# Two shared-expert blocks change their place in a two-layer mixture-of-experts kernel

## The chip, the cores and the metric

The kernel runs on one core of one Trainium2 chip. The metric is device time in microseconds of one execution. The core has a matrix engine (TensorE, PE in the profile, with its weight loads as PEld), a vector engine (VectorE, DVE), a scalar engine (ScalarE, ACT), GpSimd (POOL) and a queue that issues most DMA transfers (SyncE, SP). Each engine works through its own instructions in order and waits on semaphores for the others. Matrix products land in PSUM; everything else lives in SBUF or, for large intermediate tensors, in DRAM.

## The reference, cut to what matters

4096 tokens of width 256 go through a feed-forward layer, an attention layer and the same feed-forward layer again, each added to its input (the feed-forward layers by half). A feed-forward layer is a mixture of eight routed experts plus a shared expert that sees all tokens:

```python
logits = xn @ router_w.T                      # per token, after an RMS norm
topk_p, topk_i = jax.lax.top_k(softmax(logits), 2)
dispatch = order[:, :capacity]                # up to 640 tokens of each expert
xg = xf[dispatch]
eout = einsum('eci,eih->ech', silu(xg @ rg) * (xg @ ru), rd)   # inner width 1024
routed = zeros.at[dispatch].add(eout * weight)
shared = silu(x @ sg) * (x @ su) @ sd         # inner width 2048, all tokens
return shared + routed

x = x + 0.5 * ffn(layernorm(x))
x = x + attn(layernorm(x))                    # 16 heads, causal, groups of 64 tokens
x = x + 0.5 * ffn(layernorm(x))
```

The shared expert and the routed experts of a layer both only add to the output, so they may run in any order once their inputs are there.

## The kernel before

Tokens are cut into 32 tiles of 128 and eight blocks of 512. Weights and activations are split in two 16-bit planes (high and low), and each product is formed from three of the four combinations, so every matrix product appears three times.

**Work units.** A *front* (`front_steps`, L606) takes one tile: layer-norm statistics, the two planes into a tile `X` that also carries four numbers for routing, a DMA transpose of them into the block's `xb`, and the router's logits (L207). Phase a has ten buffers for `X` (the `10` in L751), phase c has six. After a block's fourth tile, `route` (L214) finds each token's two experts and places (`di`, L266), and `scatter` (L279) writes each of the four `X` tiles with two indirect DMAs from POOL into the experts' lists `xg` in DRAM; only then is the `X` buffer free. A *shared block* (`shared`, L349) runs the shared expert over one block of 512 tokens in 16 chunks of the inner width. A chunk is `gate_up` (L296): twelve products of 128x512 into `pgu`, the activation on ACT, a multiply on DVE, a cast to `hh` on ACT and a subtraction to `hl` on DVE. Then comes `down`: twelve products of 128x256 into `po`, put off by one chunk (`defer`), so that the chain on ACT and DVE runs beside the next chunk's products. With `tanh=True` the activation is put together from tanh with one more DVE operation[...]. After the last chunk the residual, loaded at chunk 2 by `res_load`, is added (L363) and stored (L366). The routed experts (`experts`, L389) go over eight experts in eight chunks each, with weights loaded and split on the fly, and end each expert with five scaled tiles `eo` (four buffers) that POOL adds to the output by indirect DMA (L426).

**Phases.** Phase a interleaves the 32 first-layer fronts with shared blocks 0 to 4 of the first layer (`NA = 5`). Phase b runs the first layer's experts. Phase c runs the attention tiles (`attn_tile`, L473, each with the second layer's front at its end) among shared blocks: first-layer blocks 5 to 7, then second-layer blocks 0 to 7. Phase d runs the second layer's experts, whose results are added to the output itself; the kernel ends there.

**What sets the order.** `drive` (L677) takes steps of a shared block, three for each chunk, and after every `RATE` of these lets all live tiles go on by one step, which is a slot; a tile starts every `GAP` slots. With `RATE_A = 3.0` a slot is one chunk. `run_slots` moves tiles alone when a block has to wait for its fronts. This order is then rearranged within each engine by a scheduler at build time; on the chip it is fixed. In phase a the residual rows of the blocks that are not done there are copied from `x` to `acc`, one 512 KB copy each (L764 and L765). The attention writes its result to a DRAM tensor `x2`, from which second-layer blocks load their residual.

Of the kernel before, what the change touches and what calls it, by code (L numbers as in the profile page):

```python
# [27 lines left out]
NB = 8  # L28
BT = 512
# [8 lines left out]
class Net:  # L38
# [307 lines left out]
            res.append(r)  # L346
        return res

    def shared(self, b, xb, src, dst, tanh=False, res=None):  # L349
        nc = self.nc  # L350
        outs = [self.ps_out.tile([P, BT], F32, name="po", tag="po") for _ in range(2)]
        for c in range(16):
            if c == 2 and res is None:
                res = self.res_load(src, b)
            h = self.hbuf()
            yield from self.gate_up(self.sgu[:, c], xb, h, tanh)

            def fin(c=c, h=h):
                self.down(outs, 4, h, self.sdw[:, :, c], c, 16)
                if c < 15:  # L360
                    return
                for i in range(2):
                    nc.vector.scalar_tensor_tensor(  # L363
                        out=res[i], in0=outs[i].rearrange("p (t f) -> p t f", f=H), scalar=0.5 / WS,
                        in1=res[i], op0=ALU.mult, op1=ALU.add)
                    nc.sync.dma_start(  # L366
                        out=dst[b * BT + i * 2 * P:b * BT + (i + 1) * 2 * P].rearrange("(t p) f -> p t f", p=P),
                        in_=res[i])

            self.defer(fin)  # L370
            yield
# [299 lines left out]
def run_slots(tiles, until):  # L671
    while not until():
        for _ in tiles.steps():
            pass


def drive(main, tiles, rate):  # L677

    credit = 0.0
    side = iter(())  # L680
    for _ in main:
        credit += 1.0
        for _ in range(2):
            if next(side, "end") == "end":
                break
        if credit >= rate:
            for _ in side:
                pass
            credit -= rate
            if not tiles.done():  # L690
                side = tiles.steps()
    for _ in side:
        pass


@with_exitstack
def macaron(ctx, tc, x, w_qkv, ln_w, w_proj, router_w, rg, ru, rd, sg, su, sd, out):
    nc = tc.nc
    x = x.rearrange("b s h -> (b s) h")
    out = out.rearrange("b s h -> (b s) h")  # L700
    n = Net(ctx, tc)
    R1 = n.route_init(0)
    R2 = n.route_init(1)
    R2["acc"] = out
    x2 = n.dr.tile([T, H], F32, name="x2")
    fbs = {}
    used = set()

    def new_fb(h, b):
        def get(t):  # L710
            if t == 0:
                assert h == 1 or (1, b) in used
                fb = fbs[(h, b)] = n.front_new()
                fb["pe"] = h == 1 and b < PEB
            return fbs[(h, b)]
        return get

    def tail(R, h, b, t):
        if t == 3:
            yield from n.route(R, b, fbs[(h, b)])  # L720

    def tile1(j):
        b, t = divmod(j, 4)
        y = n.load_tile(x, b, t)
        yield
        yield
        yield from n.front_steps(y, t, new_fb(1, b))
        yield from tail(R1, 1, b, t)

    def tile2(j):  # L730
        b, t = divmod(j, 4)
        yield from n.attn_tile(R1, j, x2, new_fb(2, b))
        yield from tail(R2, 2, b, t)

    def ready(h, b):
        return lambda: (h, b) in fbs and fbs[(h, b)]["n"] == 4

    def all_shared(key, b, src, dst, **k):
        yield from n.shared(b, fbs[key]["xb"], src, dst, **k)
        used.add(key)  # L740

    def fill(R):

        for e in range(E):
            z = n.raw.tile([P, 5, XW], F32, name="zero")
            nc.gpsimd.memset(z, 0.0)
            nc.vector.tensor_scalar_add(z[:, :, H], n.tokid[:, 0:5], float(T + e * CAP))
            nc.sync.dma_start(out=R["xg"][e * CAP:(e + 1) * CAP].rearrange("(t p) f -> p t f", p=P), in_=z)
            yield

    with n.phase("a", BT, 2, 10):  # L751
        n.ident = n.at.tile([P, P], F32, name="ident")
        make_identity(nc, n.ident)
        n.load_router(router_w)
        tiles = Tiles(tile1, 32, GAP_A)
        run_slots(tiles, ready(1, 0))
        n.load_shared(sg, su, sd)
        for _ in fill(R1):
            pass
        for b in range(NA):  # L760
            run_slots(tiles, ready(1, b))
            if b == 2:
                tiles.extra.append(fill(R2))
                for i in range(NA, NB):  # L764
                    nc.sync.dma_start(out=R1["acc"][i * BT:(i + 1) * BT], in_=x[i * BT:(i + 1) * BT])  # L765
            drive(all_shared((1, b), b, x, R1["acc"]), tiles, RATE_A)
        run_slots(tiles, tiles.done)
        cur = {}
        for _ in n.expert_load(R1, 0, cur):
            pass  # L770
    with n.phase("b", CAP, 3):
        n.experts(R1, rg, ru, rd, cur)
    with n.phase("c", BT, 2, 6, SLC):
        n.attn_init(w_qkv, ln_w, w_proj)
        tiles = Tiles(tile2, 32, GAP_C)
        for b in range(NA, NB):
            drive(all_shared((1, b), b, R1["acc"], R1["acc"], tanh=True), tiles, RATE_C)
        for b in range(8):
            run_slots(tiles, ready(2, b))
            drive(all_shared((2, b), b, x2, R2["acc"], tanh=True), tiles, RATE_C)  # L780
        run_slots(tiles, tiles.done)
        cur = {}
        for _ in n.expert_load(R2, 0, cur):
            pass
    with n.phase("d", CAP, 3):
        n.experts(R2, rg, ru, rd, cur)


NA = 5
RATE_A = 3.0  # L790
GAP_A = 2
RATE_C = 3.0
GAP_C = 4
# [32 lines left out]
```

## Time and profile before

Three timed runs gave a median of 1871.48 us (1870.2 to 1871.99). The profiled execution took 1875.79 us, of which 1874.1 are the span from its first to its last instruction.

| what | value |
|---|---|
| time of three runs, median | 1871.48 us |
| profiled execution, its time and its span | 1875.79 us, 1874.1 us |
| mean granted TensorE clock | 0.994 |
| matmuls | 13546 |
| first matmul of the first layer's experts | 361.45 us |
| share of the 16 DMA engines' time taken by SP's queue, by POOL's | 41.1%, 6.6% |
| HBM read and written | 80.52 MB, 52.33 MB |

The page gives a chain of waits, followed back from the last instruction. Its shares by engine say what the span was made of:

```profile
PE 57%; DVE 12%; POOL 10%; issue 9%; DMA 6%; ACT 4%; SPq 2%; POOLq 0%; DVEq 0%; ACTq 0%
```

"issue" is time in which an engine waited for nothing that the profile shows. A row of a timeline reads: start in us, length in us, engine, line, operation, output and inputs, size and count, and in brackets how long the engine was idle before and what released it.

### The profile page before, as it was taken

How to read it: one execution, taken by the hardware profiler on the slowest of the kernel's cores; microseconds unless marked ns; L12 is line 12 of the kernel's file. 1: busy time of each engine (PE TensorE's matmuls, PEld its weight loads, DVE VectorE, ACT ScalarE, POOL GpSimd, SP SyncE). 2: the span in 40 equal slices, each digit the busy share in tenths (PEclk: the TensorE clock that was granted, in tenths of full speed). 3: DMA queues.
4: the chain of work that ended last, by engine and by line, in shares of the span. 5: the costliest groups of instructions: out<-in, count | busy, mean ns of one | idle time of the engine just before them, and what ended most of it. 6: DMA issues, size and time to landing. Idle time of an engine off the chain costs nothing.

```text
span 1874.1 us, 37396 instructions
## 1 busy us (share of the span) xinstructions
PE 1786.8 (95%) x13546; PEld 1191.7 (64%) x13546; DVE 1262.5 (67%) x3190; ACT 942.1 (50%) x1991; POOL 724.5 (39%) x943
## 2 busy tenths in 40 slices
PE   6899999999999999999999999999999999999996
PEld 3455555677777765666565655656566567777775
DVE  8756554456666656788888888888886556565663
ACT  5323323355555535666566666656643335555553
POOL 5743332011112223455757667575753001111122
PEclk9999999999999999999999999999999999999998
DMA  9742113045455424556657576766631304544542
GB/s 278 220 125 75 35 29 86 21 102 115 112 113 125 104 55 86 110 105 120 139 114 141 102 141 119 135 121 119 129 62 37 86 12 102 114 113 105 117 109 50
DMA packets 447481, 196.07 MB, mean 105 GB/s; under 512 B 302353, under 2 KB 444365, under 8 KB 447248
## 3 DMA queue, kind: packets, MB, share of 16 engines
q1 hardware_dynamic: 429632, 172.51, 41.1%
q0 software_dynamic: 17664, 21.17, 6.6%
q8 instruction: 106, 1.74, 0.4%
q14 instruction: 79, 0.65, 0.1%
HBM read 80.52 MB, written 52.33 MB: 71 GB/s over the span
## 4 chain that ended last, share of the span: by engine, by line
PE 57%; DVE 12%; POOL 10%; issue 9%; DMA 6%; ACT 4%; SPq 2%; POOLq 0%; DVEq 0%; ACTq 0%
PE pgu L306 36%; PE po L330 19%; POOL xg L287 3%; DVE hl L322 2%; DVE sl L319 2%; DVE sl L314 2%; DMA xg<-X,di 1%; DMA QT<-QK 1%; DMA rs<-in_L_ffn_su_dram 1%; POOL X L285 1%; DMA y<-in_L_attn_x_dram 1%; ACT hh L321 1%; POOL e L561 1%; DVE st L139 1%; POOL S L550 1%
## 5 line engine op out<-in xcount | busy, mean ns | idle before, releaser
L306 PE MATMUL pgu<-xb,sgu 128*128 128x512 f16 x3072 | 738.8, 380 | 26.3 <-DVE sl L319 11.1
L321 ACT CAST hh<-sl 128x512 f16<-128x512 f32 (+2 forms) x512 | 272.8, 533 | 563.3 <-DVE sl L319 521.4
L306 PE MATMUL pgu<-xe,wc 128*128 128x384 f16 (+1 forms) x3072 | 497.0, 299 | 0.5
L306 PEld LDWEIGHTS <-sgu 128*128 128x128 f16 x3072 | 293.2, 98 | 301.1 <-issue 35.8
L319 DVE SCALAR_TENSOR_TENSOR sl<-pgu,sl 128x512 f32<-128x512 f32 (+2 forms) x512 | 300.2, 587 | 204.7 <-PE pgu L306 171.4
L322 DVE TENSOR_TENSOR hl<-sl,hh 128x512 f16<-128x512 f32 (+2 forms) x512 | 328.4, 642 | 154.4 <-ACT hh L321 147.5
L330 PEld LDWEIGHTS <-hh 128*128 128x128 f16 x3328 | 320.6, 98 | 115.0 <-ACT hh L321 17.9
L306 PEld LDWEIGHTS <-wc 128*128 128x128 f16 x3072 | 300.5, 98 | 94.1 <-issue 1.8
L330 PE MATMUL po<-sdw,hh 128*128 128x256 f16 x2048 | 351.9, 273 | 7.3 <-ACT hh L321 6.9
L330 PE MATMUL po<-sdw,hl 128*128 128x256 f16 x1024 | 251.9, 274 | 15.8 <-DVE hl L322 10.8
L330 PE MATMUL po<-wd,hh 128*128 128x256 f16 x1280 | 223.4, 273 | 0.0
L330 PEld LDWEIGHTS <-hl 128*128 128x128 f16 x1664 | 162.9, 98 | 67.4 <-DVE hl L322 27.2
L317 ACT ACTIVATE sl<-pgu 128x384 f32<-128x384 f32 (+1 forms) x336 | 159.0, 473 | 55.3 <-PE pgu L306 34.2
L426 POOL DMA_INDIRECT out_dram<-eo,eid x40 | 64.6, 1616 | 313.8 <-DVE hl L322 248.3
L287 POOL DMA_INDIRECT xg<-X,di x128 | 136.0, 1063 | 112.2 <-DVE di L266 54.1
L426 POOL DMA_INDIRECT acc<-eo,eid x40 | 65.1, 1627 | 285.4 <-DVE hl L322 245.8
L330 PE MATMUL po<-wd,hl 128*128 128x256 f16 x640 | 152.4, 273 | 2.1 <-DVE hl L322 2.1
L314 DVE SCALAR_TENSOR_TENSOR sl<-sl,pgu 128x512 f32<-128x512 f32 x176 | 119.9, 681 | 38.3 <-ACT sl L313 37.2
L100 ACT ACTIVATE wc<-re 128x512 f16<-128x512 f32 x128 | 80.5, 629 | 83.3 <-PE pgu L306 52.9
L313 ACT ACTIVATE sl<-pgu 128x512 f32<-128x512 f32 x176 | 103.9, 591 | 33.3 <-PE pgu L306 31.8
L101 DVE SCALAR_TENSOR_TENSOR wc<-re,wc 128x512 f16<-128x512 f32 x128 | 88.3, 690 | 26.6 <-ACT wc L100 26.4
L550 POOL TENSOR_TENSOR S<-S,amx 128x1024 f32<-128x1024 f32 x32 | 63.7, 1990 | 81.3 <-DVE amx L549 74.4
(140 smaller groups left out, 1719.6 us busy)
## 6 DMA issues: line engine op xcount, KB each, us to landing
re<-in_L_ffn_rg_dram SPq DMA_DIRECT2D x128, 128.0 KB
re<-in_L_ffn_ru_dram SPq DMA_DIRECT2D x128, 128.0 KB
re<-in_L_ffn_rd_dram SPq DMA_DIRECT2D x128, 128.0 KB
xg<-zero SPq DMA_DIRECT2D x16, 650.0 KB
y<-acc SPq DMA_DIRECT2D x64, 128.0 KB
y<-in_L_attn_x_dram SPq DMA_DIRECT2D x32, 128.0 KB
acc<-xr SPq DMA_DIRECT2D x16, 256.0 KB
x<-y SPq DMA_DIRECT2D x32, 128.0 KB
```

The costliest lines, as they stand in the source:

```text
L101: nc.vector.scalar_tensor_tensor(out=lo, in0=src, scalar=WS, in1=hi, op0=ALU.mult, op1=ALU.subtract)
L287: i = nc.gpsimd.indirect_dma_start(out=R["xg"][:, :], out_offset=bass.IndirectOffsetOnAxis(ap=di[:, t, k:k + 1], axis=0), in_=X, in_offset ...
L306: nc.tensor.matmul(p, lhsT=wc[:, w, i, k, :], rhs=x[:, 2 * a + k, :], start=(j == 0), stop=(j == 5))
L313: nc.scalar.activation(s, p, AF.Tanh, scale=0.5 / XP)
L314: nc.vector.scalar_tensor_tensor(out=s, in0=s, scalar=1.0, in1=p, op0=ALU.add, op1=ALU.mult)
L317: nc.scalar.activation(s, p, AF.Silu, scale=1.0 / XP)
L319: nc.vector.scalar_tensor_tensor(out=s, in0=ps[1], scalar=1.0 / XP / (2.0 * XP if tanh else 1.0), in1=s, op0=ALU.mult, op1=ALU.mult)
L321: nc.scalar.copy(h[0], s)
L322: nc.vector.tensor_tensor(out=h[1], in0=s, in1=h[0], op=ALU.subtract)
L330: nc.tensor.matmul(o, lhsT=h[a][:, t * P:(t + 1) * P], rhs=wd[:, w], start=(c == 0 and j == 0 and t % 2 == 0), stop=(c == nch - 1 and j == 2),
L426: i = nc.gpsimd.indirect_dma_start(out=R["acc"][:, :], out_offset=bass.IndirectOffsetOnAxis(ap=ids[:, t:t + 1], axis=0), in_=eo, in_offset ...
L550: self.anchor = nc.gpsimd.tensor_tensor(out=S, in0=S, in1=mx.unsqueeze(2).to_broadcast([P, 16, 64]), op=ALU.subtract)
```

## The change

Three things change together.

- `NA` goes from 5 to 4 and `RATE_A` from 3.0 to 2.5. Phase a keeps four shared blocks; first-layer block 4 moves to the start of phase c, where it takes the tanh form, with its residual rows copied to `acc` beforehand like those of blocks 5 to 7. A slot of phase a shrinks to 2.5 steps, 0.83 of a chunk.
- A new constant `NC = 7` leaves second-layer block 7 out of phase c and runs it in phase d, behind the routed experts and with the plain Silu form. Its residual is loaded at chunk 10 instead of 2 (`late=10`).
- The attention tiles of block 7 write their result to `out` instead of `x2`; the experts add to these rows, and the moved block loads them from `out` and stores them back. Since phase d's `h` buffers are 640 wide, `shared` cuts them to 512.

```diff
-    def shared(self, b, xb, src, dst, tanh=False, res=None):
+    def shared(self, b, xb, src, dst, tanh=False, late=2):
...
-            if c == 2 and res is None:
+            if c == late:
                 res = self.res_load(src, b)
-            h = self.hbuf()
+            h = [a[:, 0:BT] for a in self.hbuf()]
...
-        yield from n.attn_tile(R1, j, x2, new_fb(2, b))
+        yield from n.attn_tile(R1, j, x2 if b < NC else out, new_fb(2, b))
...
-        for b in range(8):
+        for b in range(NC):
             run_slots(tiles, ready(2, b))
             drive(all_shared((2, b), b, x2, R2["acc"], tanh=True), tiles, RATE_C)
...
         n.experts(R2, rg, ru, rd, cur)
+        for b in range(NC, NB):
+            for _ in all_shared((2, b), b, out, out, late=10):
+                pass
...
-NA = 5
-RATE_A = 3.0
+NA = 4
+NC = 7
+RATE_A = 2.5
```

## The prediction, made before the changed kernel ran

> **What bounds the kernel now.** I read the page's busy times first, then the rows by slice, then busy time by stage, then the end and the first stage in order of time.
>
> ```profile
> PE 1786.8 (95%) x13546; PEld 1191.7 (64%) x13546; DVE 1262.5 (67%) x3190; ACT 942.1 (50%) x1991; POOL 724.5 (39%) x943
> ```
>
> TensorE is busy for 95% of the span and no other engine for over 67%. So the time is TensorE's work plus its gaps, 87.3 us in all. The table by stage (columns: stretch, its length, then busy time and instructions of PE, PEld, DVE, ACT, POOL, granted clock, DMA share, GB/s) shows where these are. The stretches are phase a, b, c, d and what follows the last matmul.
>
> ```profile
> 0.00:363.00 363.00, 328.78 (x2062) 192.86 (x2063) 210.87 (x735) 124.12 (x227) 143.96 (x282) 0.99 0.40 110
> 363.00:683.00 320.00, 319.58 (x2529) 247.11 (x2527) 193.88 (x419) 168.25 (x398) 59.91 (x42) 1.00 0.46 104
> 683.00:1544.00 861.00, 827.48 (x6489) 510.40 (x6489) 665.46 (x1622) 483.14 (x974) 454.45 (x574) 1.00 0.54 104
> 1544.00:1857.20 313.20, 311.01 (x2471) 241.29 (x2468) 191.36 (x415) 165.78 (x393) 58.40 (x41) 1.00 0.46 106
> 1857.20:1874.10 16.90, 0.00 (x0) 0.00 (x0) 0.89 (x2) 0.83 (x2) 7.75 (x5) 0.61 0.36 39
> ```
>
> The gaps are 34.2 us in a (15.4 of them in the first 25 us), 0.4 in b, 33.5 in c, 2.2 in d, and 16.9 behind the last matmul. The two expert phases are full; only a, c and the end have anything to give.
>
> **The moved blocks.** A shared block is 16 chunks of 24 matmuls. The chain of waits shows the same group of a bare chunk return every 3.90 us:
>
> ```profile
> 336.92 2.16 PE pgu L306 x10
> 340.82 2.16 PE pgu L306 x10
> ```
>
> So a block is 16 x 3.90 = 62.4 us of TensorE. Phase a loses one (block 4), c loses one (2,7) and gains one (1,4), d gains one. The matmuls are the same in number and shape: the sum is 0. Phase c keeps eleven blocks, all with the tanh form, for 32 attention tiles. In the built programs every engine's sequence from the attention weights to the last expert is the same one instruction by instruction, except for names of tensors (the residual of one block now comes from `acc` instead of `x2`, four stores go to `out`). Last logits stand 25.5 chunks ahead of phase d's start in both. So I cost b and c at 0: their stalls stay, among them the two per block that c shows around each route.
>
> **The end.** Today the last matmul ends at 1857.2, and five scatters leave POOL one by one:
>
> ```profile
> 1857.81 1.55 POOL L426 DMA_INDIRECT out_dram<-eo,eid  x1 [27.70 <-DVE eo L425]
> 1859.67 1.54 POOL L426 DMA_INDIRECT out_dram<-eo,eid  x1 [0.30 <-issue]
> ...
> 1861.69 0.48 DVE L425 TENSOR_SCALAR eo<-po,ew 128x256 f32<-128x256 f32 x1 [4.08 <-DMA out_dram<-eo,eid]
> ...
> 1865.22 1.56 POOL L426 DMA_INDIRECT out_dram<-eo,eid  x1 [0.31 <-issue]
> ```
>
> They are issued by 1866.8 and the span ends 7.3 us later, at 1874.1. In the changed kernel they stand under the appended block. Its own end is two residual adds and two stores:
>
> ```profile
> L363 DVE SCALAR_TENSOR_TENSOR xr<-po,xr x32: 678/681/692, 99.4 to 1543.2; 128x512 f32<-128x512 f32 x32
> ```
>
> ```profile
> 1012.20 2.63 DMA out_dram<-xr
> ```
>
> The three numbers behind the colon are the shortest, median and longest add in ns; the second line is a landing of such a store in the chain of waits.
>
> The first add starts about 0.4 us before the last matmul ends (four matmuls of the other half follow its operand), so the second ends 1.0 us after; issue 0.4, landing 2.6, and 1.4 for the closing waits and barriers (0.6 of waits on SP and 0.75 from POOL's last drain to the end, by today's trace): 5.4 us instead of 16.9, **-11.5**. Bounds of the end: 4 us if the second store lands faster, 12 if POOL's closing drain, which today ends 6.5 us behind its last scatter, comes on top; it should be over, since POOL has by then been idle for some 50 us. The last chunk has no successor to hide its chain (multiply 0.69, cast 0.62, subtract 0.64 against 1.3 us of the earlier down products): **+0.4**.
>
> **Expert to shared block in d.** Expert 7's fifth `eo` has to wait for the first scatter's landing (4.08 us above; four buffers), and DVE is in order: the `sl` and `hl` of chunk 1 stand behind it. TensorE can run on for about a chunk on the three PSUM tiles of `pgu`. Nearest rows: between experts, with the same wait, TensorE loses 0 to 1.2 us; at the start of c, experts to a tanh block, 2.6. Silu has one DVE operation less than tanh, so between: **+1.5**, ends 0 and 4. The residual load at chunk 10 waits on SP for all scatters; only the two final stores are queued behind it, and 39 us have gone by against some 12 for five scatters: 0.
>
> **The denser front (phase a).** Rate 2.5 puts 28 fronts and eight routes over 50 chunks instead of 60; TensorE's cover for them shrinks, the work stays. What stalls today is a ring: each tile takes one of ten `X` tiles, and its cast on ACT waits until the tile ten before it was scattered.
>
> ```profile
> ACT X L164 <- DMA xg<-X,di: 25.4, 14, 3.0
> PE pgu L306 <- DVE sl L319: 9.0, 8, 2.5
> ```
>
> The columns are us in total, waits, and the longest. The casts wait 25.4 us on ACT, and TensorE is idle for 12.6 us from 75 to 250. From the first scatter's start to the release of tiles 0 to 3 of a block takes 4.0, 6.5, 9.1 and 11.6 us (165.78 to the casts at 169.75 and 172.31, then two scatters of 1.28 each per tile): 1.0, 1.7, 2.3, 3.0 chunks. The built order puts the casts 2,2,3,3 chunks behind `di` for tiles 10-13 and 14-17, 1,2,2,3 for the next three groups, 1,2 for tiles 30 and 31. After: 3,4,4,4; 1,2,2,3; 1,1,2,2; 1,2,2,3; 1,2,3,3; 1,1. The largest shortfall per group sums to 0.9 chunks before and 2.3 after: 1.4 chunks, 5.5 us more of ACT waiting. By today's ratio 12.6 / 25.4 half of it reaches TensorE: +2.8.
>
> Here a rule weighs in. TensorE is granted half its clock for windows of 3.4 us:
>
> ```profile
> 105.61 0.59 PE L306 MATMUL pgu<-xb,sgu 128*128 128x512 f16 x2 [2.00 <-DVE sl L319]
> 147.75 1.03 PE L330 MATMUL po<-sdw,hh 128*128 128x256 f16 x4 [0.28 <-ACT hh L321]
> ```
>
> Four products take 1.03 us at 147.75, behind a wait of 2.51, and 0.60 elsewhere; the granted clock is 0.93 from 100 to 125. The Trainium skill ("TensorE: Matmul & The Clock Gate", section "HAM oscillation — how this bites in real kernels") puts the danger at idle gaps above about 3.4 us. By the rule, longer waits of 2 to 3 us cost only themselves: +2.8. By the row a wait of 2.0 to 2.5 already loses half a window, 1.7 us. Not each does: 1.91 us at 686.75 was followed by full clock. I go by the row and allow 0.4 of one more window, 0.7. Phase a: **+3.5**. Low end -3 (stalls such as 105.61, where DVE waited for a load of `y`, need not recur); high end +14, the second rival below. One more 512 KB copy to `acc` is issued near 29 us, where the DMA engines are full (share 1.16): 1.8 us at 287 GB/s, but TensorE is busy throughout that slice, so 0 within these ends.
>
> At the end of a the last `di` stands 11 chunks ahead of the first expert instead of 17: 43 us. Today the last block's scatters start at 297.4 and the weights of the first two expert chunks are split by 323.7, so 26.3 suffice: 16 spare, and ACT's order puts the first split 4 chunks behind `di` in both.
>
> **Sum.** -11.5 + 0.4 + 1.5 + 3.5 = -6.1. Against the profiled span of 1874.1 (its run took 1875.8, 1.7 around it) that is 1868.0; the median of the runs, 1871.5, becomes **1865.4**. A change under 0.2%, 3.7 us, can't be told from none.
>
> **Rivals.**
> - *The front costs nothing* (0.20): a neutral or better a, -1, leaves -10.6: 1860.9. For it: groups 10-13 get more slack, and the scheduler placed the order knowing the rate. Against: groups 18-21 and 30-31 get less.
> - *Gain given back* (0.18): 4 at the expert boundary and 7 in a: -11.5 + 0.4 + 4 + 7 = -0.1, 1871.4. For it: DVE is in order behind a 4 us wait, at a place no trace shows.
> - *The X ring becomes the bound* (0.16), the slower side. Place: the casts on ACT behind the scatters. If each of five groups adds a wait of 2.5 us and a half-clock window of 1.7, a grows by 21: 1871.5 - 9.6 + 21 = 1882.9. It decides from 13.3 us in a (9.6 of gain and 3.7). For it: POOL takes a fixed 10 us for eight scatters, while a block's turn (8 slots, of 1 chunk before and 0.83 after) falls from 31 to 26 us. Against: 26 still holds them, with DVE at 27 of 50 us and DMA at 0.23 share from 200 to 250.
> - That the experts start late is inside the last: it takes over 16 us of slip.
>
> The forecast itself has 0.46, from 1862 to 1868. Faster: 0.46 + 0.20 = 0.66; same 0.18; slower 0.16. Range 1859 to 1877: below lies little of the second case, above about two thirds of the slower one.
>
> **What would show it.** Last matmul to end: near 5.4 us. First expert matmul near 361.5 - 62.4 + 3.5 = 302.6. Phases b and c as long as now, within 2 us. TensorE's gap at the expert boundary 0 to 4 us. I am wrong if a keeps more than 13 us of its 62.4, if c changes length, or if a POOL drain still follows the last store.

## The result

Four timed runs of the changed kernel have a median of 1853.26 us (1851.16 to 1854.37), four of the kernel before 1870.84. The ratio is 0.9907, with a 95% interval of 0.9895 to 0.992: 17 us faster, and 6 us below the lower end of the predicted range. A second set of runs gave the unaltered changed kernel 0.9924 (0.9911 to 0.9937), which is 14 us; one of its six runs, 2309.23 us at a granted clock of 0.753, is a slow one and left out. So the gain lies between 14 and 17 us where 6.1 were forecast.

The profiled execution took 1854.02 us, its span is 1852.2. The page's busy times, and the first of its shares of the chain of waits:

```profile
PE 1785.9 (96%) x13546; PEld 1189.7 (64%) x13546; DVE 1259.6 (68%) x3190; ACT 940.6 (51%) x1991; POOL 726.0 (39%) x943
...
PE 59%; DVE 11%; POOL 9%; DMA 8%; issue 6%; ACT 4%; SPq 1%; DVEq 0%; POOLq 0%; ACTq 0%
```

TensorE does the same 13546 matmuls in the same time. Its gaps were 87.3 us of the span and are 66.3. The table by stage of the changed kernel, with phases a, b, c, d, the appended block, and what follows the last matmul:

```profile
0.00:292.00 292.00, 264.46 (x1667) 153.82 (x1668) 183.87 (x700) 103.42 (x194) 145.43 (x282) 0.99 0.50 134
292.00:607.00 315.00, 314.86 (x2505) 244.40 (x2503) 192.73 (x415) 166.64 (x394) 58.43 (x41) 1.00 0.46 105
607.00:1466.00 859.00, 826.67 (x6476) 508.43 (x6475) 665.01 (x1622) 482.29 (x973) 455.93 (x574) 1.00 0.53 104
1466.00:1783.00 317.00, 315.39 (x2505) 244.28 (x2503) 192.72 (x416) 167.83 (x395) 58.32 (x41) 1.00 0.45 105
1783.00:1847.90 64.90, 64.56 (x401) 38.73 (x399) 24.39 (x38) 20.41 (x35) 7.89 (x5) 1.00 0.12 19
1847.90:1852.20 4.30, 0.00 (x0) 0.00 (x0) 0.86 (x2) 0.00 (x0) 0.00 (x0) 0.86 0.37 122
```

The gaps are now 27.5 us in a (34.2 before), 0.1 in b, 32.3 in c (33.5), 1.6 in d, 0.3 in the appended block and 4.3 at the end (16.9). Two places gave the time: the end and phase a. With the stages cut at the first and last gate or up product of each layer's experts, the two profiled executions stand like this:

| stretch | before, us | after, us | difference | predicted |
|---|---|---|---|---|
| a: start to the first expert product | 361.45 | 291.84 | -69.6 = -62.4 - 7.2 | -62.4 + 3.5 |
| b: first layer's experts | 315.4 | 314.9 | -0.5 | 0 |
| c | 860.8 | 859.0 | -1.8 | 0 |
| d: second layer's experts | 317.3 | 316.9 | -0.4 | 0 |
| last gate or up product of an expert to the end | 19.1 | 69.5 | +62.4 - 12.0 | +62.4 - 9.6 |

The pair of profiles differs by 21.8 us, 4 to 8 more than the timed runs. The profiled execution before was a long one: its 1875.79 us lie above all four timed runs of its kernel here (1868.89 to 1871.99). The chip counts too: the four sets of experiments, each on another chip, put the median of the kernel before at 1868.48, 1867.83, 1871.1 and 1876.16 us, and on which chip this profile was taken is not on record. So times are compared within a set only, and part of the -7.2 in phase a may belong to that one execution, which the experiments have to settle.

**The end.** The last rows of the changed kernel in order of time (start, length, engine and line, operation, and in brackets the idle time before and what ended it):

```profile
1846.10 0.61 PE L330 MATMUL po<-sdw,hh 128*128 128x256 f16 x4 [0.20 <-ACT hh L321]
...
1847.47 1.29 DVE L363 SCALAR_TENSOR_TENSOR xr<-po,xr 128x512 f32<-128x512 f32 x2 [0.70 <-PE po L330]
...
1847.60 0.27 PE L330 MATMUL po<-sdw,hl 128*128 128x256 f16 x1
1848.19 0.98 SPq L366 DMA_DIRECT2D out_dram<-xr  x2
```

No POOL instruction stands here any more. The last matmul ends at 1847.87, the two adds at 1848.8, the second store is issued and landed, and the span ends 4.28 us behind the last matmul instead of 16.9. The last chunk's bare chain costs the 0.20 in the first row.

**Experts to the shared block in d.** The same view where the last scatters now run:

```profile
1787.45 3.83 PE L306 MATMUL pgu<-xb,sgu 128*128 128x512 f16 x17
1788.15 1.70 POOL L426 DMA_INDIRECT out_dram<-eo,eid  x1 [30.44 <-DVE eo L425]
...
1792.16 0.48 DVE L425 TENSOR_SCALAR eo<-po,ew 128x256 f32<-128x256 f32 x1 [3.75 <-DMA out_dram<-eo,eid]
1792.43 0.81 PE L306 MATMUL pgu<-xb,sgu 128*128 128x512 f16 x3
```

DVE does wait 3.75 us for the first scatter with its fifth `eo`, but TensorE runs 17 gate and up products in one go under it and shows no wait at all. Its three PSUM tiles of cover were enough.

### The profile page after: what moved, and what is told of

The parts are those of the page before. It is cut to its first block, busy times and chain, and to the rows that moved or that the text cites. A ratio compares the mean times of both kernels' runs of the same rounds, so it can differ in the third digit from the quotient of the medians.

```text
span 1852.2 us, 37412 instructions
## 1 busy us (share of the span) xinstructions
PE 1785.9 (96%) x13546; PEld 1189.7 (64%) x13546; DVE 1259.6 (68%) x3190; ACT 940.6 (51%) x1991; POOL 726.0 (39%) x943
## 4 chain that ended last, share of the span: by engine, by line
PE 59%; DVE 11%; POOL 9%; DMA 8%; issue 6%; ACT 4%; SPq 1%; DVEq 0%; POOLq 0%; ACTq 0%
PE pgu L306 38%; PE po L330 19%; POOL xg L287 3%; DVE hl L322 2%; DVE sl L319 2%; DMA xg<-X,di 2%; DVE sl L314 2%; DMA xg<-zero 1%; DMA y<-in_L_attn_x_dram 1%; DMA rs<-in_L_ffn_su_dram 1%; POOL X L285 1%; ACT hh L321 1%; DMA QT<-QK 1%; DVE st L139 1%; ACT V L554 1%
```

## The experiments

Two theories stood against each other at first. *Ring*: phase a pays for its density through the ten `X` tiles, so the surplus must come from elsewhere. *Front*: the denser front itself gains. The edits are against the kernel named with each. Ratios are to the kernel before on the same chip, in the same set of runs.

### First set: the parts of the change one by one

**front_only.** The kernel before with the denser front alone.

```diff
-RATE_A = 3.0
+RATE_A = 2.5
```

> The kernel before with RATE_A 2.5 alone; five blocks stay in phase a, eight second-layer blocks in phase c. The prediction's theory (the ring of X tiles makes a denser front dearer): phase a longer by 3.5 us, so about 1874. Rival one (the gaps of phase a come once per front or route and are bounded by what TensorE meets there, so that fewer chunks beside fronts means fewer gaps): phase a shorter by 3 to 7 us, 1864 to 1868. Rival two (phase a's gaps vary from run to run and the rate means nothing): within 2 us of before.

Measured 1866.68 us, ratio 0.9988 (0.998 to 0.9997): a gain of 2 us, at the limit of what can be told. The +3.5 of the forecast had the wrong sign; a gain of 3 to 7 was too much as well.

**no_late_block.** The changed kernel with block 7 back in phase c.

```diff
-NC = 7
+NC = 8
```

> The changed kernel with NC 8: four blocks in phase a and the denser front, but all eight second-layer blocks in phase c, so the kernel ends with the last expert's scatters as before. If the end is worth the 11.5 to 12.6 us that the two traces show, this runs 12 to 13 us slower than the changed kernel, 1865 to 1866, and what is left against before (5 us) belongs to phase a. If the late block gains by something else as well (phase c being shorter at its end), the difference is larger.

Measured 1865.76 us, ratio 0.9982 (0.9975 to 0.9989): 3 us for the whole front part. Against the changed kernel's 0.9907 and 0.9924 the appended block is thus worth 14 or 11 us; its trace ends 19.1 us behind the last expert product, as before.

**late_only.** The changed kernel with phase a as it was.

```diff
-NA = 4
+NA = 5
...
-RATE_A = 2.5
+RATE_A = 3.0
```

> The changed kernel with NA 5 and RATE_A 3.0: phase a as before, block (2,7) moved behind the experts, ten blocks left in phase c. The end gains 12 us as in the changed kernel. Phase c loses a block of cover: the last logits stand 9.5 chunks (37 us) ahead of the second experts instead of 25.5, and route, scatters and expert load took some 35 us in the trace of before. If that cover suffices, 1858 to 1859; if it falls short, TensorE is idle at the start of phase d by 5 to 15 us and the time is 1863 to 1873.

Measured 1858.33 us, ratio 0.9954 (0.994 to 0.9968), a gain of 9 us by the ratio and 10 by the medians. Its trace has the changed kernel's end (69.6 us behind the last expert product). But its phase a, the same order of work as before, took 356.72 us where the profile before shows 361.45. TensorE's idle time in phase a was 34.2 us there and is 32.4 here, and a window of half clock comes three times there and once here. So one execution can make 4.7 of the -7.2 by itself, and 2.5 are left for the change.

**four_slow_front.** The changed kernel with the old rate.

```diff
-RATE_A = 2.5
+RATE_A = 3.0
```

> The changed kernel with RATE_A 3.0: four blocks in phase a but the front as thin as before. The last di stands one chunk ahead of the first experts instead of 11, and 26 us pass from the last scatters to the split weights, so TensorE is idle for about 20 us at the end of phase a: 1853 + 20 = 1873, give or take 5. If it stays within 5 us of 1853, the denser front was not needed to move the block.

Measured 1873.09 us, ratio 1.0027 (1.0016 to 1.0038): slower than before. Its table by 25 us, in the columns of the table by stage:

```profile
275.00:300.00 25.00, 21.67 (x145) 13.35 (x142) 12.71 (x47) 6.53 (x11) 6.65 (x17) 1.00 0.07 22
300.00:325.00 25.00, 10.22 (x62) 6.49 (x63) 6.20 (x15) 5.66 (x13) 4.93 (x7) 0.66 0.60 129
```

and in order of time TensorE's row where the experts begin:

```profile
314.53 5.84 PE L306 MATMUL pgu<-xe,wc 128*128 128x384 f16 x26 [17.54 <-ACT wc L100]
```

With 16 chunks less to hide under and the old spacing, the fronts outlast the shared blocks; TensorE stands for 17.5 us. The 0.66 is the mean of the slice, the wait included: in shorter slices the granted clock is 0.50 from 305 to 318 us, that is for about the first 4 us of the experts' work, which costs another 2 us (an estimate: half of these 4). The denser front is no gain worth having alone. It is what lets four blocks be enough, and that is worth some 20 us. The prediction's reading that the experts start in time at the rate of 2.5 holds: the changed kernel is busy for 24.5 of the 25 us from 275 to 300.

### Second set: is the ring a bound?

The view of waits from 45 to 300 us shows, for the changed kernel (columns: total us, times, longest):

```profile
ACT X L164 <- DMA xg<-X,di: 41.5, 20, 5.4
```

ACT's casts waited 25.4 us for `X` tiles before and wait 41.5 now, +16 where 5.5 were worked out. Two other traces show that density alone did not make this. The first row is late_only, whose engines go through phase a in the same order as the kernel before, instruction by instruction; the second is front_only:

```profile
ACT X L164 <- DMA xg<-X,di: 34.6, 18, 3.2
ACT X L164 <- DMA xg<-X,di: 35.6, 21, 4.2
```

So 9 of the 16 us lie between two executions of one order, and the denser front by itself stands only 1 us above the higher of them. The 41.5 belongs to four blocks with the dense front (41.5 in no_late_block too, 44.5 in after_again). If half of it reached TensorE, a longer ring should bring some 20 us.

**after_x32.** All 32 tiles get their own `X` buffer.

```diff
-    with n.phase("a", BT, 2, 10):
+    with n.phase("a", BT, 2, 32):
```

> The changed kernel with 32 X tiles in phase a instead of ten, so that no cast on ACT waits for a scatter (41.5 us of such waits in the trace of the changed kernel). The prediction's theory, that half of these waits reaches TensorE: about 20 us faster than the changed kernel, 1833. Rival (the ring's waits lie in ACT's idle time, and TensorE's chain of cast and subtraction has room for them): within 3 us of the changed kernel; TensorE's gaps from 50 to 125 us stay as they are.

Measured 1849.33 us, ratio 0.9895 (0.988 to 0.9909), with the unaltered changed kernel at 1854.2 and 0.9924 beside it (after_again, the second set named in the result):

> The changed kernel unaltered, as the measure for the three beside it on the same chip: 1853 within 2 us, of which the end gives 12 to 13 and phase a 2 to 3.

The ring costs about 5 us, by the two intervals 2 to 9: not 20, and more than the rival's 3 only by the medians. after_x32 is the fastest kernel of the study and beats both versions.

**after_x8.** The ring cut to eight, against the changed kernel.

```diff
-    with n.phase("a", BT, 2, 10):
+    with n.phase("a", BT, 2, 8):
```

> The changed kernel with eight X tiles instead of ten. The built order puts the casts 1 to 3 chunks behind the di of the tile eight before, as short as with ten, and two tiles later. The prediction's theory: the largest shortfalls, by its own table of 1.0, 1.7, 2.3 and 3.0 chunks, stay 0.3 to 1.0 for each group and there is one group more, so 2 to 4 us slower. Rival: within 3 us, either side.

Measured 1855.71 us, ratio 0.993 (0.9917 to 0.9942): 1.5 us more than with ten, which the intervals don't tell from none. Two tiles less hardly matter; the ring is no cliff.

**rate20.** Denser still.

```diff
-RATE_A = 2.5
+RATE_A = 2.0
```

> The changed kernel with RATE_A 2.0: the last logits at chunk 40 of 64 instead of 50. If a denser front shortens phase a because TensorE meets its gaps in fewer chunks, another 2 to 4 us, 1849 to 1851. If the prediction's ring is what a denser front costs, 3 to 6 us slower, 1856 to 1859. If the gaps come from loads and stores early in phase a that no rate moves, within 1.5 us of 1853.

Measured 1858.08 us, ratio 0.9941 (0.9929 to 0.9954), 3 to 4 us worse than at 2.5. That is the time which the ring's theory gave, but not by the ring: ACT's ring waits fell to 31.7 us while phase a grew to 297.3. In this trace less waiting on ACT went with more loss on TensorE; the loss sits from 75 to 125 us, where TensorE is idle for 10.3 us.

### Third and fourth set: where does a thin front lose?

At the end of phase a TensorE has a gap in every order. Its rows there in the kernel before, in order of time:

```profile
316.70 1.46 PE L306 MATMUL pgu<-xb,sgu 128*128 128x512 f16 x6 [1.60 <-DVE sl L319]
...
318.92 0.61 PE L330 MATMUL po<-sdw,hh 128*128 128x256 f16 x4 [0.77 <-ACT hh L321]
```

and the largest one in front_only:

```profile
271.76 0.61 PE L330 MATMUL po<-sdw,hh 128*128 128x256 f16 x4 [0.59 <-ACT hh L321]
```

DVE and ACT wait there, in order, for the first expert's tags and weights, and the shared block's chain stands behind. The stretch from 250 us to the first expert product, in the columns of the table by stage, of the kernel before, late_only and front_only:

```profile
250.00:361.45 111.45, 108.66 (x679) 64.47 (x677) 47.90 (x121) 34.54 (x59) 21.26 (x42) 1.00 0.16 37
250.00:356.72 106.72, 102.27 (x638) 60.78 (x637) 44.84 (x109) 32.86 (x56) 19.66 (x31) 1.00 0.17 38
250.00:353.45 103.45, 102.26 (x626) 60.92 (x625) 39.79 (x64) 32.91 (x56) 8.60 (x10) 1.00 0.16 39
```

TensorE is idle there for 2.8, 4.5 and 3.8 us with the thin front and five blocks (before, late_only, before_x32), and for 1.2 to 1.5 with the dense one (front_only, no_late_block, the changed kernel, after_again); that would explain front_only's 2 us. Weights loaded ahead and the first expert's tags taken later were tried against it, and the ring was taken away under the thin front too.

**after_prefetch, before_prefetch.** The first expert chunk's weights of each layer are loaded ahead into tiles of their own, in the changed kernel and in the kernel before.

```diff
+    def prefetch(self, rg, ru, rd):
+        r = self.pre.tile([P, 2, 2, P], F32, name="pre1")
+        for i, s in enumerate((rg, ru)):
+            self.nc.sync.dma_start(out=r[:, i], in_=s[0, :, 0:P].rearrange("(k p) f -> p k f", p=P))
+        r2 = self.pre.tile([P, H], F32, name="pre2")
+        self.nc.sync.dma_start(out=r2, in_=rd[0, 0:P])
+        self.first = r, r2
...
+                if e == 0 and c == 0:
+                    r, r2 = self.first
...
+            if b == NA - 1:
+                n.prefetch(rg, ru, rd)
             drive(all_shared((1, b), b, x, R1["acc"]), tiles, RATE_A)
...
+            if b == NC - 1:
+                n.prefetch(rg, ru, rd)
             drive(all_shared((2, b), b, x2, R2["acc"], tanh=True), tiles, RATE_C)
```

> The changed kernel with the weights of each layer's first expert chunk loaded ahead of time into tiles of their own, so that the first split on ACT, near the end of phases a and c, no longer waits for them (5.9 us of ACT waiting and 1.3 us of TensorE's in phase a of the changed kernel, 1.4 us of TensorE's in the gap at the end of c). Theory (this in-order wait on ACT is what phase a still loses at its end): 2 to 3 us faster than the changed kernel's 1853 to 1854, so about 1851. Rival (the wait only moves to the second chunk's weights): within 1 us.

> The same prefetch in the kernel before, where the wait of the first split takes 2.9 us from TensorE in the trace of before and 4.3 in that of the run with the late block alone, both with the thin front. Theory (the denser front gained its 2 us there, at the end of phase a): 3.5 to 5.5 us faster than before, more than the prefetch gives the changed kernel. Rival (the denser front gains in the stretch of the fronts themselves): the same 2 to 3 us as in the changed kernel.

Measured 0.9926 (0.9913 to 0.994) and 1.0018 (1.0011 to 1.0024): no gain, and a loss of 0.2% on the kernel before, which neither theory had. TensorE's largest gap at that place in after_prefetch:

```profile
278.39 1.46 PE L308 MATMUL pgu<-xb,sgu 128*128 128x512 f16 x6 [1.73 <-DVE sl L321]
```

It is larger than the changed kernel's (0.93, and 1.21 in after_again). DVE still waits there for the tags, 3.88 us at 271.48 (4.66 us at 269.41 in the changed kernel), so the chain may stand behind the tags whether the weights are there or not.

**before_x32.** The kernel before with 32 `X` buffers.

```diff
-    with n.phase("a", BT, 2, 10):
+    with n.phase("a", BT, 2, 32):
```

> The kernel before with 32 X tiles, so without the ring. In the changed kernel this gave 5 us. The prediction's theory (a denser front makes the ring dearer): clearly less here, 0 to 2 us. Rival (the ring costs the same at either rate, since the scheduler lets the fronts run ahead until the ring is full, whatever the rate): again 4 to 6 us.

Measured 1863.13 us, ratio 0.9957 (0.9943 to 0.997), a gain of 8 us, by the interval 6 to 11. So the ring is not cheaper under the thin front, as the forecast of 0 to 2 us had it. That it is dearer there, 8 us against 5, is not shown: the two intervals overlap. The tables by 50 us from 125 on show where the ring costs. First the kernel before, then late_only, which has the same order:

```profile
125.00:175.00 50.00, 46.13 (x296) 27.05 (x294) 27.56 (x100) 14.62 (x27) 22.52 (x37) 0.97 0.25 68
175.00:225.00 50.00, 48.53 (x322) 29.45 (x321) 30.61 (x123) 16.73 (x31) 19.85 (x47) 1.00 0.25 64
...
125.00:175.00 50.00, 49.24 (x329) 29.85 (x328) 30.10 (x108) 15.99 (x31) 24.40 (x41) 1.00 0.34 91
175.00:225.00 50.00, 48.33 (x321) 29.01 (x320) 30.02 (x120) 16.92 (x31) 18.13 (x43) 1.00 0.18 42
```

then the changed kernel:

```profile
125.00:175.00 50.00, 48.70 (x325) 29.21 (x323) 35.10 (x146) 17.20 (x32) 24.19 (x54) 1.00 0.31 86
175.00:225.00 50.00, 49.10 (x336) 30.11 (x334) 28.90 (x119) 16.90 (x31) 22.69 (x48) 1.00 0.15 37
```

then the changed kernel with 32 buffers:

```profile
125.00:175.00 50.00, 50.00 (x333) 30.01 (x331) 30.37 (x124) 16.58 (x30) 23.54 (x48) 1.00 0.21 64
175.00:225.00 50.00, 50.00 (x343) 30.64 (x341) 26.05 (x111) 15.50 (x26) 21.17 (x41) 1.00 0.04 12
```

TensorE is busy for 94.7 of these 100 us in the one trace of the thin order and 97.6 in the other, 97.8 in the changed kernel and 100 without the ring (100 in before_x32 too). What the ring costs TensorE shows here under both fronts, and two executions of one order differ by as much as the two fronts do. By the first expert product the ring costs 4.9 us from late_only to before_x32, and 5.7 and 4.7 from the changed kernel and after_again to after_x32: about the same.

**best_three.** The changed kernel with 32 buffers, the weights ahead, and the zero fill of the second lists a block later.

```diff
+            if b == 3:
+                tiles.extra.append(fill(R2))
             if b == 2:
-                tiles.extra.append(fill(R2))
```

> The changed kernel with 32 X tiles, the prefetch, and the zero fill of the second layer's lists started one block later (b == 3), out of the stretch from 50 to 125 us in which TensorE still loses some 10 us while the DMA engines are 40 to 110% busy. If the first two add up, 1849.3 - 2.5 = 1847; if the fill is part of those 10 us, 1842 to 1845; if the fill collides with the scatters instead, 1848 or more.

Measured 1854.6 us, ratio 0.9915 (0.9902 to 0.9929): no better than after_x32's 0.9895; the two intervals touch. What is added to the 32 buffers brings nothing.

**before_late_ids, after_late_ids, x32_late_ids.** As the prefetch kernels, with the first expert's tags and weights by token taken in its fourth chunk; on the kernel before, the changed kernel, and the changed kernel with 32 buffers.

```diff
+                if e == 0 and c == 3:
+                    for _ in rest:
+                        pass
+                    ids, wts = own["id"], own["w"]
...
-        for _ in n.expert_load(R1, 0, cur):
-            pass
+        rest = n.expert_load(R1, 0, cur)
+        next(rest)
```

> The same in the kernel before, where this gap is 3 to 4 us with the thin front. If the denser front of the changed kernel gained its 2 us by this gap, the gap falls under 1 us here too and the time is 3 to 4 us below the prefetch alone (1871 instead of 1874.6), so that before and changed front then differ by under 1 us in phase a. If the denser front gained elsewhere, the two keep their distance of 2 us or more.

> The changed kernel with the prefetch and with the first expert's token numbers and weights (the POOL cast and two DVE operations that wait for the list's tags) taken in the expert's fourth chunk; the scheduler then puts them one chunk later than now. Prefetch alone did nothing, since DVE waits for the tags just where ACT waits for the weights. If these two waits together make the gap near the end of phase a, the gaps of 1.3 us (changed kernel) and 2.2 us (prefetch alone) fall under 0.5 us, and the time is 1 to 3 us below the prefetch alone, 1854 to 1856 by that run. If not, the gap moves on once more and the time stays at 1857.

> The changed kernel with 32 X tiles, the prefetch and the late token numbers, with the zero fill where it was. If the gap at the end of phase a is gone and the prefetch costs nothing early on, 1 to 2 us below 32 tiles alone, 1847 to 1848; if the prefetch in the busy first 50 us is what cost the combination of three its gain, 1851 to 1854.

Measured 1.0024 (1.0013 to 1.0035), 0.991 (0.9896 to 0.9923) and 0.9909 (0.9896 to 0.9922). None beats its own base by more than the noise. The build placed the tags at the end of phase a again: in before_late_ids DVE waits 5.97 us for them, and TensorE's row shows one gap larger than before:

```profile
327.73 2.72 PE L308 MATMUL pgu<-xb,sgu 128*128 128x512 f16 x6 [3.58 <-DVE sl L321]
```

So no experiment took this gap away. That a dense front gains 2 us at the end of phase a is read from the traces and not shown by a run that changes it alone.

## Why the prediction was wrong

Its direction was right, and so was the largest term. The time fell below the range mainly because of one step in phase a. The three signs of being wrong that it named did not come: phase a gave up more than its 62.4 us, c kept its length within 2 us, and no POOL drain follows the last store. All three watched the slow side.

- **The end, -11.5.** Right. The traces give 12.6 behind the last matmul: POOL's closing drain is gone, as expected, and the last stores came to the end in 4.28 us instead of 5.4. The timed runs give 9 (late_only) to 14 (no_late_block against the first set) for the end and the boundary together, where the sum had 9.6.
- **The last chunk, +0.4, and the boundary in d, +1.5.** Too dear. The chain costs 0.20, and TensorE never waited under the `eo` wait. By the table of stretches both, with all else in d's last 65 us, come to 0.6 (12.6 - 12.0). Of the two rows that it was set between, that between experts (0 to 1.2 us) was the nearer, and not the start of c (2.6).
- **b and c at 0.** Right within 2 us, as stated; c was 859.0 and 859.8 in the two traces of the changed kernel, 860.8 before.
- **Phase a, +3.5. This is the step that failed: "By today's ratio 12.6 / 25.4 half of it reaches TensorE: +2.8."** Its sign was wrong: by the timed runs the front part is worth -2 us (front_only), -3 with block 4 moved as well (no_late_block), and -6 to -9 where late_only is set against the changed kernel. The runs show three faults in the step.
  - *The count of waits.* The shortfalls give 0.9 chunks, 3.5 us, for the order before, where its own trace has 25.4 us of ring waits. And the 5.5 us worked out for the change are less than the 9 by which these waits differ in two executions of the order before (25.4 and 34.6).
  - *The ratio.* TensorE's 12.6 us from 75 to 250 were not the ring's alone: 4.9 of idle time stay there without it (before_x32). In late_only 34.6 us of ring waits go with only 10.0 us of idle time in that stretch. More waiting on ACT went with less on TensorE, in the same order of work.
  - *A term at nothing.* For the end of phase a, where the experts' first loads stand in ACT's and DVE's order, the sum has no term. There TensorE's idle time is 2.8 to 4.5 us with the thin front and 1.2 to 1.5 with the dense one. This has the size of front_only's gain, but it is read from traces; why the dense front loses less there, and what else it gains, stays open.
- **The clock, +0.7.** Wrong in the count; that a wait of about 2 us can be followed by half clock was right. The rows of the changed kernel (TensorE from 76 to 104 us, clock windows beginning at 76.1 and 100.0):

```profile
76.16 2.72 PE L306 MATMUL pgu<-xb,sgu 128*128 128x512 f16 x6 [2.43 <-ACT sl L317]
...
98.38 0.61 PE L330 MATMUL po<-sdw,hh 128*128 128x256 f16 x4 [1.88 <-ACT hh L321]
...
101.68 2.30 PE L306 MATMUL pgu<-xb,sgu 128*128 128x512 f16 x6
```

  Six products of 128x512 take 2.72 and 2.30 us here and 1.46 elsewhere, again behind waits of only 1.9 to 2.4 us, so the row was the better guide than the rule of the Trainium skill ("TensorE: Matmul & The Clock Gate", section "HAM oscillation — how this bites in real kernels"), which sets the danger at gaps above 3.4 us. But there are two such windows in phase a where there were three, not one more; and late_only, in the order of the kernel before, has one, so the count is not the order's alone.
- **The rivals.** "The front costs nothing" was the nearest and still 7.6 us too slow, since it gave phase a a gain of only 1 us and kept the 9.6 of the end with its 1.9 us for chunk and boundary. The ring as the bound is refuted by after_x32.

The terms as the runs give them, 11 to 14 for the end by no_late_block and 3 for the front part, sum to the 14 to 17 us measured. The two are not independent of it: no_late_block's ratio splits the measured gain, and it can't say where within 11 to 14 the end lies. The trace's 12.0 does. Split by late_only instead, the gain is 9 for the end and 6 to 9 for the front. Open remain whether the two parts give more together (14 to 17 us) than each alone (9 and 3, by their intervals up to 15), why the thin front loses more, and the idle time of 4 to 10 us from 75 to 125 us, which all orders of phase a have in some measure.

## What to carry to other kernels

A wait on an engine that does not bound the time has no fixed price: in two executions of one order of work such waits were 25.4 and 34.6 us, and the bounding engine was idle for 12.6 and 10.0 us. So read the gaps of the bounding engine in that stretch, or take the resource away in an experiment, before converting one into the other. Where a kernel ends with scatters from GpSimd, put work behind them that needs neither them nor GpSimd and leaves by plain stores; here that alone was worth 9 to 14 us. And where a forecast is made from one profiled execution, first ask how far that execution lies from the median and in which stage: here one stage differed by 4.7 us between two executions, more than the whole term of 3.5.

## What the hardware showed beyond expectation

- The same order of phase a took 361.45 us in one execution and 356.72 in another (before and late_only), with three half-clock windows in the one and one in the other. Two windows of 3.4 us at half clock are 3.4 us of lost work (an estimate), the larger part of the 4.7; TensorE's idle time makes 1.8. Whether the chip or chance made the difference is not shown, since the chip of the first is not on record.
- Behind the single wait of 17.5 us (four_slow_front) the granted clock stayed at 0.50 for about 4 us of the work that followed: more was lost than the wait. The waits of about 2 us were followed by half-clock windows as well, of about 3.4 us (76.1 to 79.5 us and 100.0 to 103.4 in the changed kernel).
